# Running sums of the keys' exponentials: from a triangular product on TensorE to a prefix scan on VectorE, with one product of v moved

## The chip, the cores and the metric

The kernel runs on one core of a Trainium2 chip. The metric is the device time of one execution in microseconds (us); lower is better. Within the core, TensorE (PE in the profile; PEld is its weight load), VectorE (DVE), ScalarE (ACT), GpSimd (POOL) and the DMA queues (issued by SyncE, SP) work side by side, each through its own instructions in order, and wait for each other by semaphores.

## The reference

The input has 2 batches of 2048 tokens with 512 features. A gated attention with 64 slots per head (16 heads, key width 64, value width 128) is followed by a layer norm, a gated feed-forward part with a Hadamard transform, and another layer norm. What the change touches is the attention's gating:

```python
z = cumlogsumexp(s, axis=time)            # s = clip(x @ Ws, -32, 32)
g = exp(z[t-1] - z[t])                    # decay of the state
p = exp(s - z)                            # weight of the new token
hk = hk * g + k * p;   ok = q . hk        # keys' state, 64 x 64 per head
pv = softmax(ok)
hv = hv * g + p * v;   ov = pv . hv       # values' state
o = rmsnorm(ov) * gn * silu(x @ Wg);  out = o @ Wo
```

The kernel writes E = exp(s) and keeps the states unscaled. The running sum over time Z of E then enters only as a factor 1/Z on the scores ok and again on the softmax's result. So each chunk of tokens needs Z at every token and slot, its reciprocal, and the last Z of the chunk for the next chunk.

## The kernel before

The attention part walks over `NG` = 4 groups of four heads, and in each over 16 chunks of 128 tokens, both batches together: 64 steps (`Step`). The feed-forward part follows. All is in fp32.

One call of `run` works on four steps at once: `new` loads its input, `now` does its projections and keys' part, `before` does its values' part, and `old` finishes its output product and stores its rows. The kernel writes out the order of PE, DVE, ACT and POOL by hand (a manual schedule), so `run`'s body is the order in each engine's queue, as far as each line uses that engine.

The projections are Strassen-like: a product is seven smaller ones, numbered 1 to 7. `q(k)` makes q, k and s, `v(k)` makes v and the gate, `o(k)` is the output product of an older step. Each accumulates in PSUM banks called `c1` (products 1, 6, 7, 4), `c2` (5, 3) and `c3` (2); `into` then moves a sum out, by ACT (copies `kept`, line 458, and `t`, 460) or by DVE (line 463). For `o`, DVE adds each sum to `rows` (line 742). In a step there are thus two bursts of large products, the seven of q and then v(6), v(5), v(2), v(7), v(3), v(4), with `o` products among them, and between the bursts lies the attention with its small products:

- `exp_s`: DVE clamps s (511); ACT makes `e` (517), and, except in the first chunk of a group, a second exponential `e2` (515), to whose first row POOL adds `zc`, the last running sums of the chunk before (516).
- `k_transposed` (549, copy `kr` 551), `scores` (580), `scores2` (655), `share_of_keys` (590), `share_of_values` (667), `e_transposed` (555, copy `eT` 557), `slots` (608), `state_slots` (617), `values` (678), `state_values` (687).
- `running_sum`: PE multiplies E with a triangular matrix `causal` (562), in a bank of the `c1` kind; ACT copies the result to `z` (564), and two DMAs carry its last row to `zc`. Its second half of columns has the two halves of the tokens swapped (`causal3`).
- `reciprocal` in two halves on DVE (573), each 128x256, one ahead of the values' part, one within v's burst.
- `gated`: ACT squares the values' result (704), DVE multiplies (706) and sums (708), POOL scales (710 to 713).
- `softmax`: DVE multiplies the scores with 1/Z into `r` (625), takes the maximum (631) and subtracts (633); ACT takes the exponential (634). `softmax_sum` sums on DVE and multiplies with 1/Z on POOL (640).
- `o_transposed`: PE transposes (730), ACT copies to `ob` (427, 428), DVE makes two differences (432, 433). Then `o(1)`, `o(5)`, `o(2)` run, and the next call of `run` begins with its q burst.

In the last group, `row_stats` (lines 86 to 91) and `normalize` (95) are done on an old step's rows, the second `row_stats` and `normalize` right after `running_sum`.

The part of the order in `run` that the change touches is, before:

```python
do(now, "exp_s");  ...;  main("v", 1);  ...
do(now, "k_transposed");  do(old, "o", 4);  ...
do(now, "e_transposed");  do(now, "running_sum")
```

Of the kernel before, what the change touches and what calls it, by code (L numbers as in the profile page):

```python
# [9 lines left out]
F32 = mybir.dt.float32  # L10
AF = mybir.ActivationFunctionType
ALU = mybir.AluOpType
# [3 lines left out]
P = 128  # L16
# [5 lines left out]
M = 64  # L22
HG = 4
NG = H // HG
NQ = 4
TH = P // 2
HALVES = (slice(0, TH), slice(TH, P))
# [11 lines left out]
def gated_slot_attention_ffn_kernel(  # L39
# [13 lines left out]
    nc = tc.nc  # L53
# [6 lines left out]
    const = ctx.enter_context(tc.tile_pool(name="const", bufs=1))  # L60
    small = ctx.enter_context(tc.tile_pool(name="small", bufs=4))
    ident = const.tile([P, P], F32, name="ident")
    make_identity(nc, ident)


    causal3 = const.tile([P, P + TH], F32, name="causal")
    causal = causal3[:, 0:P]
    make_upper_triangular(nc, causal, val=1.0, diag=True)
    nc.gpsimd.tensor_copy(causal3[:, P:], causal3[:, 0:TH])
    mhalf = const.tile([P, 2 * NQ], F32, name="mhalf")  # L70
    nc.gpsimd.memset(mhalf, -0.5)
    gn = const.tile([P, 1], F32, name="gn")
# [51 lines left out]
    pch = ctx.enter_context(tc.tile_pool(name="pch", bufs=1, space=PSUM))  # L124
# [23 lines left out]
    xb, acc, res, h, wt = {}, {}, {}, {}, []  # L148
# [203 lines left out]
    with ExitStack() as att:  # L352
        keep = att.enter_context(tc.tile_pool(name="keep", bufs=1))
        c2 = att.enter_context(tc.tile_pool(name="c2", bufs=2))
        c1 = att.enter_context(tc.tile_pool(name="c1", bufs=1))
# [7 lines left out]
        def bank(at, width=P):  # L363
            return ps[at // 2][:, at % 2].rearrange("p (i t) -> p i t", t=width)
# [15 lines left out]
        hk = [keep.tile([P, NQ, M], F32, name=f"hk{s}") for s in range(3)]  # L380
        hv = [keep.tile([P, NQ, DV], F32, name=f"hv{s}") for s in range(2)]

        zc = keep.tile([1, NQ, P], F32, name="zc")
        xd = [dram.tile([P, 7, 2, P], F32, name=f"xd{n}") for n in range(NCB)]

        QUARTERS = [(i, j, HALVES[j], s, HALVES[s], HALVES[s ^ j]) for i in range(NQ) for j in range(2) for s in range(2)]
        OPENS = (1, 2, 5)

        def settle(sums):

            nc.scalar.copy(small.tile([P, 1], F32, name="seen", bufs=1), sums)
# [71 lines left out]
        class Step:  # L465
# [31 lines left out]
            def multiply_q(self, out, k):  # L497
                wt = w["qks"].t
                for c in range(2):
                    xk, wk_ = self.xb[:, RIGHT[k], c, :], wt[:, LEFT[k], c, :]  # L500
                    for i in range(3):
                        a, b = (wk_[:, i * P : (i + 1) * P], xk) if i < 2 else (xk, wk_[:, 2 * P :])
                        nc.tensor.matmul(  # L503
                            out[:, i * P : (i + 1) * P], lhsT=a, rhs=b,
                            start=(k in OPENS and c == 0 and i == 0), stop=(c == 1), skip_group_check=True,
                        )

            def exp_s(self):

                self.e = self.e2 = c2.tile([P, NQ, P], F32, name="e")  # L510
                nc.vector.tensor_scalar(self.e, self.t1[:, :, 2 * P :], -CLAMP, CLAMP, ALU.max, ALU.min)
                if not self.first:

                    self.e2 = c1.tile([P, NQ, P], F32, name="e2", tag="e2")
                    nc.scalar.activation(self.e2, self.e, AF.Exp)  # L515
                    nc.gpsimd.tensor_tensor(self.e2[0:1], self.e2[0:1], zc, ALU.add)  # L516
                nc.scalar.activation(self.e, self.e, AF.Exp)


# [7 lines left out]
            def multiply_v(self, out, k):  # L527
                for c in range(2):
                    nc.tensor.matmul(  # L529
                        out, lhsT=self.xb[:, RIGHT[k], c, :], rhs=w["vg"].t[:, LEFT[k], c, :],  # L530
                        start=(k in OPENS and c == 0), stop=(c == 1), skip_group_check=True,
                    )
# [24 lines left out]
                nc.scalar.copy(self.eT.rearrange("p (j i) t -> p j i t", j=2), pe)  # L557

            def running_sum(self):
                p = pch.tile([P, 512], F32, name="running", tag="c1", bufs=2).rearrange("p (i t) -> p i t", t=P)  # L560
                for j, h in enumerate(HALVES):
                    nc.tensor.matmul(p[:, :, h], lhsT=(causal, causal3[:, TH:])[j], rhs=self.e2[:, :, h], start=True, stop=True)
                z = c1.tile([P, NQ, P], F32, name="z", tag="z")
                nc.scalar.copy(z, p)  # L564
                self.z = z
                if not self.final:
                    for at, h in zip((P - 1, TH - 1), HALVES):
                        nc.sync.dma_start(out=zc[:, :, h], in_=z[at : at + 1, :, h])
                self.iz = c1.tile([P, NQ, P], F32, name="iz")

            def reciprocal(self, half):
                h = slice(2 * half, 2 * half + 2)
                nc.vector.reciprocal(self.iz[:, h], self.z[:, h])  # L573


            def scores(self):
# [119 lines left out]
            def gated(self):  # L696

                sq = c1.tile([P, 2, NQ, DV], F32, name="sq", tag="big")
                self.gj = self.t2[:, :, HD:].rearrange("p q (j d) -> p j q d", d=DV)

                every = slice(0, P)
                moves = [(0, every, every), (1, HALVES[0], HALVES[1]), (1, HALVES[1], HALVES[0])]
                for j, to, at in moves:
                    nc.scalar.activation(sq[to, j], self.po[j][at], AF.Square)  # L704
                for j, to, at in moves:
                    nc.vector.tensor_tensor(self.gj[to, j], self.po[j][at], self.gj[to, j], ALU.mult)  # L706
                ss = small.tile([P, 2 * NQ], F32, name="ss")
                nc.vector.tensor_reduce(ss, sq.rearrange("p j q d -> p (j q) d"), AX.X, ALU.add)  # L708
                self.state()
                nc.gpsimd.tensor_scalar(ss, ss, 1.0 / DV, EPS, ALU.mult, ALU.add)  # L710
                nc.gpsimd.tensor_tensor(ss, ss, mhalf, ALU.pow)
                ssb = ss.rearrange("p (j q o) -> p j q o", j=2, o=1).to_broadcast([P, 2, NQ, DV])
                nc.gpsimd.tensor_tensor(self.gj, self.gj, ssb, ALU.mult)
# [30 lines left out]
            def multiply_o(self, out, k):  # L744
                for c in range(2):
                    nc.tensor.matmul(  # L746
                        out, lhsT=self.ob[:, RIGHT[k], c, :], rhs=w["o"].t[:, LEFT[k], c, :],
                        start=(k in OPENS and c == 0), stop=(c == 1), skip_group_check=True,
                    )
# [248 lines left out]
        def run(new, now, before, old):  # L998


            def do(step, name, *args):
                if step is not None:
                    getattr(step, name)(*args)

            def main(name, k):

                if now is not None:
                    getattr(now, name)(k)
                elif before is not None:
                    for _ in range(FILL[name, k]):  # L1010
                        next(ups)

            def work_on(place):

                if not changes:
                    y["place"] = place
                    next(pieces[0], None)
# [5 lines left out]
            def more():  # L1023

                if old is not None and old.g == NG - 1 and old.n >= NCB - 4:
                    work_on(1)
# [47 lines left out]
                f(0)  # L1074
            if opens:
                w["vg"] = nw.pop("vg")
            main("v", 1)
            more()
            do(before, "load_rows")
            do(now, "k_transposed")  # L1080
            do(old, "o", 4)
# [9 lines left out]
            do(now, "share_of_keys")  # L1091
            do(before, "share_of_values")
            do(now, "e_transposed")
            do(now, "running_sum")
            do(old, "row_stats", 0)
            do(old, "normalize")
# [26 lines left out]
            if o_last:  # L1123
                nw["o"].sums(0, nc.gpsimd)
                nw["o"].sums(1, nc.gpsimd)
            main("v", 7)
            do(now, "softmax")
            main("v", 3)
            more()
# [32 lines left out]
        with tc.manual_schedule(  # L1162
            engines={mybir.EngineType.PE, mybir.EngineType.DVE, mybir.EngineType.Activation, mybir.EngineType.Pool}
        ):
            steps[0].load_x()
            nw["qks"] = load_qks(0)
            steps[1].load_x()
            nw["vg"] = load_vg(0)
            nw["o"] = load_o(0)
            steps[0].make_x()  # L1170
            for k in range(4):
                nw["qks"].sums(k)
            N = len(steps)
            for i in range(N + 2):
                if i == N:
                    open_x("wvg", OUTER[3:], 4 * P)
                    open_acc("ux", tag="h1")
                    ups = up(0, h)
                run(*(steps[j] if 0 <= j < N else None for j in (i + 1, i, i - 1, i - 2)))
            for _ in pieces[0]:  # L1180
                pass
# [6 lines left out]
    with tc.manual_schedule(  # L1188
# [11 lines left out]
        for u in range(NU):  # L1200
            if u:
                h = {}
# [89 lines left out]
```

## Time and profile before

| what | value |
|---|---|
| median of 3 runs | 3518.95 us (3515.03 to 3519.06) |
| profiled execution, its own time | 3517.86 us |
| profiled execution, span from first to last instruction | 3516.1 us |
| busy in the span: TensorE / VectorE / ScalarE / GpSimd | 98% / 67% / 27% / 33% |
| granted TensorE clock, mean | 0.999 |
| running sum on TensorE (line 562) | 256 records of 0.379 us |
| its copy by ScalarE (564) | 64 of 0.587 us |
| reciprocals on VectorE (573) | 128 of 1.75 us |
| GpSimd's additions of zc (516) | 60 of 1.27 us |

The attention part takes about the first 2440 us, the feed-forward part the rest. Busy time is a share of the span. A record of a matmul reaches from its start to a modelled end, and the next one starts before that end; so what a product takes of TensorE's queue is the distance from its start to the next start.

### The profile page before, as it was taken

What the parts mean: (1) busy time and instruction counts of PE and PEld (TensorE: products, weight loads), DVE (VectorE), ACT (ScalarE), POOL (GpSimd) and SP (SyncE); (2) the same over time, 40 slices, a digit from 0 to 9 for tenths busy, and PEclk for the clock granted to TensorE, in tenths of its full rate; (3) what the DMA queues carried; (4) which work ended last, traced back from release to release, by engine and by line L of the source; (5) the groups of instructions that cost most, each with busy time, mean ns of one, the idle gap of its engine ahead of it and who ended that gap; (6) DMA issues with size and microseconds to landing.
All of it is one profiled execution on the core that took longest, in us unless ns stands there. A gap on an engine that the chain in (4) does not pass through costs nothing. (4 is left out here: it accounts for less than half of the span.)

```text
span 3516.1 us, 75258 instructions
## 1 busy us (share of the span) xinstructions
PE 3456.7 (98%) x31840; PEld 2702.8 (77%) x31840; DVE 2354.9 (67%) x3940; ACT 957.0 (27%) x1712; POOL 1144.2 (33%) x1069
## 2 busy tenths in 40 slices
PE   8999999999999999999999999998999999999998
PEld 6777777677777677677777777776888888888887
DVE  5777776665666765656766677777666756756756
ACT  3333333333333333333333333332111111111110
POOL 1222223221221331221332222223634643643544
PEclk9999999999999999999999999999999999999999
DMA  5334334221122232122222243347555544445431
GB/s 184 118 113 138 118 119 152 93 72 62 55 66 70 94 96 65 52 66 70 74 99 68 69 140 129 102 160 270 171 179 205 174 161 176 156 151 184 163 135 68
DMA packets 208833, 425.03 MB, mean 121 GB/s; under 512 B 19696, under 2 KB 120432, under 8 KB 207472
## 3 DMA queue, kind: packets, MB, share of 16 engines
q1 hardware_dynamic: 208496, 420.22, 35.7%
q8 instruction: 250, 4.10, 0.5%
q14 instruction: 87, 0.71, 0.1%
HBM read 297.47 MB, written 125.30 MB: 120 GB/s over the span
## 5 line engine op out<-in xcount | busy, mean ns | idle before, releaser
L529 PE MATMUL c<-wvg,xb 128*128 128x512 f32 x1792 | 812.7, 598 | 4.0 <-DVE wvg L412 2.0
L529 PEld LDWEIGHTS c<-wvg,xb 128*128 128x128 f32 x1792 | 322.1, 190 | 369.6 <-issue 291.9
L503 PE MATMUL c<-xb,wqks 128*128 128x128 f32 x3584 | 553.2, 277 | 15.7 <-DMA wqks<-wqks_blocks 9.6
L503 PEld LDWEIGHTS c<-xb,wqks 128*128 128x128 f32 x3584 | 479.9, 193 | 43.7 <-DVE rows L742 21.5
L218 DVE TENSOR_TENSOR accux<-c,accux 128x512 f32<-128x512 f32 x496 | 341.4, 691 | 180.9 <-PE c L237 163.5
L276 PE MATMUL dc<-w2t,hid 128*128 128x256 f32 x1792 | 455.3, 379 | 2.1 <-DVE res L283 2.1
L237 PE MATMUL c<-wvg,xb 128*128 128x256 f32 x1792 | 432.0, 380 | 6.1 <-DVE accux L218 5.3
L742 DVE TENSOR_TENSOR rows<-c,rows 128x256 f32<-128x256 f32 x448 | 181.7, 418 | 335.9 <-PE c L746 331.4
L237 PEld LDWEIGHTS c<-wvg,xb 128*128 128x128 f32 x1792 | 338.8, 190 | 56.9 <-DVE accux L218 9.1
L276 PEld LDWEIGHTS dc<-w2t,hid 128*128 128x128 f32 x1792 | 340.2, 190 | 49.5 <-DVE res L283 3.3
L503 PE MATMUL c<-wqks,xb 128*128 128x128 f32 x1792 | 347.4, 276 | 0.0
L463 DVE TENSOR_TENSOR t<-c,kept 128x384 f32<-128x384 f32 (+1 forms) x384 | 230.6, 611 | 155.6 <-PE c L503 147.5
L237 PE MATMUL c<-wqks,xb 128*128 128x256 f32 x1344 | 325.1, 380 | 5.2 <-DVE accux L218 2.3
L458 ACT COPY kept<-c 128x384 f32<-128x384 f32 (+1 forms) x384 | 203.5, 530 | 457.8 <-PE c L503 369.5
L516 POOL TENSOR_TENSOR e<-e,zc 1x512 f32<-1x512 f32 x60 | 76.4, 1273 | 710.0 <-ACT e L515 710.0
L237 PEld LDWEIGHTS c<-wqks,xb 128*128 128x128 f32 x1344 | 253.9, 190 | 44.0 <-DVE accux L218 5.0
L503 PEld LDWEIGHTS c<-wqks,xb 128*128 128x128 f32 x1792 | 273.0, 193 | 0.0
L283 DVE TENSOR_TENSOR res<-dc,res 128x256 f32<-128x256 f32 x448 | 189.2, 423 | 117.9 <-PE dc L276 107.3
L573 DVE RECIPROCAL iz<-z 128x256 f32<-128x256 f32 x128 | 223.9, 1749 | 44.6 <-ACT z L564 44.6
L710 POOL TENSOR_SCALAR ss<-ss 128x8 f32<-128x8 f32 x64 | 12.7, 198 | 685.3 <-DVE ss L708 685.3
L706 DVE TENSOR_TENSOR t<-po,t 64x512 f32<-64x512 f32 (+1 forms) x192 | 131.6, 685 | 95.6 <-ACT sq L704 94.3
L252 POOL TENSOR_TENSOR accw<-accw,accux 128x512 f32<-128x512 f32 x64 | 80.8, 1276 | 275.7 <-DVE accux L218 274.3
(189 smaller groups left out, 4975.7 us busy)
## 6 DMA issues: line engine op xcount, KB each, us to landing
xb<-w13s SPq DMA_DIRECT2D x112, 896.0 KB
xb<-xd SPq DMA_DIRECT2D x48, 896.0 KB
yd<-rows SPq DMA_DIRECT2D x128, 256.0 KB
w2t<-w2s SPq DMA_DIRECT2D x32, 896.0 KB
rows<-yd SPq DMA_DIRECT2D x100, 256.0 KB
xd<-xb SPq DMA_DIRECT2D x16, 896.0 KB
wvg<-fxd SPq DMA_DIRECT2D x16, 896.0 KB
w13s<-inner SPq DMA_DIRECT2D x96, 128.0 KB
```

What stands on the lines that cost most here:

```text
L218: nc.vector.tensor_tensor(into[:, b], s, (into if first is None else first)[:, b], ALU.add)
L237: nc.tensor.matmul(s[:, j * TQ : (j + 1) * TQ], lhsT=w[:, LEFT[k], j, :], rhs=right[:, RIGHT[k], :], start=(k in (1, 2, 5) and j == 0), st ...
L252: (nc.gpsimd if u or m == 6 else nc.vector).tensor_tensor(o, o, t["u"][:, b], ALU.add)
L276: nc.tensor.matmul(s, lhsT=h["hid"][:, i, LEFT[m], k * P : (k + 1) * P], rhs=h["w2"][:, i, RIGHT[m], :], start=(m in (1, 2, 5) and i == 0) ...
L283: nc.vector.tensor_tensor(r, s, r, ALU.add)
L458: nc.scalar.copy(self.kept[k], s)
L463: nc.vector.tensor_tensor(t[:, to], s, self.kept[other], ALU.add)
L503: nc.tensor.matmul(out[:, i * P : (i + 1) * P], lhsT=a, rhs=b, start=(k in OPENS and c == 0 and i == 0), stop=(c == 1), skip_group_check=True,
L529: nc.tensor.matmul(out, lhsT=self.xb[:, RIGHT[k], c, :], rhs=w["vg"].t[:, LEFT[k], c, :], start=(k in OPENS and c == 0), stop=(c == 1), sk ...
L573: nc.vector.reciprocal(self.iz[:, h], self.z[:, h])
L706: nc.vector.tensor_tensor(self.gj[to, j], self.po[j][at], self.gj[to, j], ALU.mult)
L742: nc.vector.tensor_tensor(y_, self.uo.sum(k), y_, ALU.add)
```

## The change

The running sums are no longer a product. The transposes of E, which the kernel makes anyway (`eT`, slots on partitions, tokens along the row), are scanned along the tokens by VectorE: `tensor_tensor_scan` computes state = state * 1 + E, once per pair of heads and batch (four instructions of 128x128 each), and starts from `zl`, the last sums of the chunk before, one number per partition. The reciprocals are taken of these transposed sums (`izT`) by the same two instructions as before. Four transposes on TensorE turn them back (`sums_transposed`, put between v(7) and v(3)), and ScalarE copies them to `iz` in three pieces, which swaps the two halves of the tokens for the second half of the columns. ScalarE also copies `zl`. Out go the second exponential, GpSimd's addition, the product with `causal`, ScalarE's copy of `z`, and the two DMAs per step. v(1) moves from ahead of `k_transposed` to behind `e_transposed`.

```diff
             def exp_s(self):
-                self.e = self.e2 = c2.tile([P, NQ, P], F32, name="e")
+                self.e = c2.tile([P, NQ, P], F32, name="e")
                 nc.vector.tensor_scalar(self.e, self.t1[:, :, 2 * P :], -CLAMP, CLAMP, ALU.max, ALU.min)
-                if not self.first:
-                    self.e2 = c1.tile([P, NQ, P], F32, name="e2", tag="e2")
-                    nc.scalar.activation(self.e2, self.e, AF.Exp)
-                    nc.gpsimd.tensor_tensor(self.e2[0:1], self.e2[0:1], zc, ALU.add)
                 nc.scalar.activation(self.e, self.e, AF.Exp)
...
             def running_sum(self):
-                p = pch.tile([P, 512], F32, name="running", tag="c1", bufs=2).rearrange("p (i t) -> p i t", t=P)
-                for j, h in enumerate(HALVES):
-                    nc.tensor.matmul(p[:, :, h], lhsT=(causal, causal3[:, TH:])[j], rhs=self.e2[:, :, h], start=True, stop=True)
-                z = c1.tile([P, NQ, P], F32, name="z", tag="z")
-                nc.scalar.copy(z, p)
-                self.z = z
-                if not self.final:
-                    for at, h in zip((P - 1, TH - 1), HALVES):
-                        nc.sync.dma_start(out=zc[:, :, h], in_=z[at : at + 1, :, h])
-                self.iz = c1.tile([P, NQ, P], F32, name="iz")
+                self.z = z = c1.tile([P, NQ, P], F32, name="z", tag="z")
+                for i in range(NQ):
+                    nc.vector.tensor_tensor_scan(
+                        z[:, i], ones, self.eT[:, i], 0.0 if self.first else zl[:, i : i + 1], ALU.mult, ALU.add
+                    )
+                self.izT = c1.tile([P, NQ, P], F32, name="izT", tag="e2")
             def reciprocal(self, half):
                 h = slice(2 * half, 2 * half + 2)
-                nc.vector.reciprocal(self.iz[:, h], self.z[:, h])
+                nc.vector.reciprocal(self.izT[:, h], self.z[:, h])
+                if half and not self.final:
+                    nc.scalar.copy(zl, self.z[:, :, P - 1])
+            def sums_transposed(self):
+                for i in range(NQ):
+                    nc.tensor.transpose(bank(0)[:, i, :], self.izT[:, i, :], ident)
+                self.iz = c1.tile([P, NQ, P], F32, name="iz")
+                for j, to, at in MOVES:
+                    m = slice(j * M, (j + 1) * M)
+                    nc.scalar.copy(self.iz[to, :, m], bank(0)[at, :, m])
...
                 w["vg"] = nw.pop("vg")
-            main("v", 1)
-            more()
             do(before, "load_rows")
             do(now, "k_transposed")
             do(old, "o", 4)
...
             do(now, "e_transposed")
+            main("v", 1)
+            more()
             do(now, "running_sum")
             do(old, "row_stats", 0)
             do(old, "normalize")
...
             main("v", 7)
+            do(now, "sums_transposed")
             do(now, "softmax")
             main("v", 3)
```

`MOVES` is the list of three moves that `gated` had of its own: all partitions for the first half of the columns, and the two halves of the partitions crossed for the second.

More of the change, by code (lines that the diff above doesn't have):

```diff
@@ L63, in gated_slot_attention_ffn_kernel @@
     make_identity(nc, ident)
-    causal3 = const.tile([P, P + TH], F32, name="causal")
-    causal = causal3[:, 0:P]
+    causal = const.tile([P, P], F32, name="causal")
     make_upper_triangular(nc, causal, val=1.0, diag=True)
-    nc.gpsimd.tensor_copy(causal3[:, P:], causal3[:, 0:TH])
+    ones = const.tile([P, P], F32, name="ones")
+    nc.gpsimd.memset(ones, 1.0)
     mhalf = const.tile([P, 2 * NQ], F32, name="mhalf")
@@ L381, in gated_slot_attention_ffn_kernel @@
         hv = [keep.tile([P, NQ, DV], F32, name=f"hv{s}") for s in range(2)]
-        zc = keep.tile([1, NQ, P], F32, name="zc")
+        zl = keep.tile([P, NQ], F32, name="zl")
         xd = [dram.tile([P, 7, 2, P], F32, name=f"xd{n}") for n in range(NCB)]
@@ L389, in gated_slot_attention_ffn_kernel @@
         OPENS = (1, 2, 5)
+        MOVES = [(0, slice(0, P), slice(0, P)), (1, HALVES[0], HALVES[1]), (1, HALVES[1], HALVES[0])]
         def settle(sums):
@@ L699, in gated @@
                 self.gj = self.t2[:, :, HD:].rearrange("p q (j d) -> p j q d", d=DV)
-                every = slice(0, P)
-                moves = [(0, every, every), (1, HALVES[0], HALVES[1]), (1, HALVES[1], HALVES[0])]
-                for j, to, at in moves:
+                for j, to, at in MOVES:
                     nc.scalar.activation(sq[to, j], self.po[j][at], AF.Square)
-                for j, to, at in moves:
+                for j, to, at in MOVES:
                     nc.vector.tensor_tensor(self.gj[to, j], self.po[j][at], self.gj[to, j], ALU.mult)
```

## The prediction

> **What bounds the kernel now.** I read the page's first rows, then the busy times by stretch, the waits, and three pieces of the timeline.
>
> ```profile
> span 3516.1 us, 75258 instructions
> PE 3456.7 (98%) x31840; PEld 2702.8 (77%) x31840; DVE 2354.9 (67%) x3940; ACT 957.0 (27%) x1712; POOL 1144.2 (33%) x1069
> ...
> 700.00:1300.00 600.00, 595.08 (x6709) 440.09 (x6708) 387.57 (x602) 201.96 (x379) 152.87 (x137) 1.00 0.23 73
> ```
>
> The last line is a stretch of attention: 600 us, then the busy time of PE, PEld, DVE, ACT, POOL, and PE's granted clock (1.00). PE is busy for 595 of 600. The attention part ends near 2440 us; the change touches nothing after it. So the currency is PE's queue: an instruction taken from it is worth its issue time, and a new wait at its head costs its whole length. The waits view says where PE's slack is thin:
>
> ```profile
> PEld c L746 <- ACT ob L427: 47.8, 64, 2.1
> ```
>
> In all 64 steps the weight load of o's first product waits for ScalarE's copy ob (47.8 us in all). That is the weight loader, not yet PE, but nothing is left between them. Now a step of the second group around q's and v's bursts; columns are start, duration, engine, line:
>
> ```profile
> 1470.70 1.03 PE L746 MATMUL c<-wo__11903,ob 128*128 128x256 f32 x4
> 1471.57 1.88 PE L529 MATMUL c<-wvg,xb 128*128 128x512 f32 x4
> 1471.77 0.42 DVE L742 TENSOR_TENSOR rows<-c,rows 128x256 f32<-128x256 f32 x1 [1.65 <-PE c L746]
> ...
> 1473.29 0.60 PE L549 MATMUL ps<-ident,t 128*128 128x128 f32 x4
> 1473.72 1.03 PE L746 MATMUL c<-wo__11903,ob 128*128 128x256 f32 x4
> 1474.68 0.69 PE L580 MATMUL ps<-t 64*64 64x64 f32 x32
> ...
> 1477.26 0.66 PE L555 MATMUL ps<-ident,e 128*128 128x128 f32 x4
> 1477.75 1.03 PE L562 MATMUL running<-e,causal 128*128 128x256 f32 x4
> ...
> 1478.71 0.46 PE L608 MATMUL ps<-e,a 64*64 64x64 f32 x16
> ```
>
> PE durations overlap (the end is modelled), so I cost PE by start to next start: o(7) 0.87, v(1) 1.72, k's transposes 0.43, o(4) 0.96, e's transposes 0.49, the running sum 0.96. DVE finishes reading o(7)'s sum at 1472.19, 1.49 after o(7) began; v(1) hides this. The same step's end:
>
> ```profile
> 1487.91 1.75 DVE L573 RECIPROCAL iz<-z 128x256 f32<-128x256 f32 x1
> 1489.57 1.22 DVE L463 TENSOR_TENSOR t<-c,kept 128x512 f32<-128x512 f32 x2
> 1490.71 0.68 DVE L625 TENSOR_TENSOR r<-ps,iz 128x512 f32<-128x512 f32 x1
> ...
> 1492.94 0.63 ACT L634 ACTIVATE r<-r 128x512 f32<-128x512 f32 x1 [5.84 <-DVE r L633]
> 1493.47 0.57 ACT L427 COPY ob<-ps 128x512 f32<-128x512 f32 x1
> ...
> 1494.10 2.86 PE L746 MATMUL c<-wo__11903,ob 128*128 128x256 f32 x12
> ```
>
> DVE runs back to back into r; ScalarE's exponential waits for r, the copy ob is queued behind that exponential, and o(1) starts 0.06 after ob ends (1494.04). o(1) is also exactly one product (1.72) after v(4)'s start: two chains end together. Last, a step of group 3, where rows are normalized too:
>
> ```profile
> 2115.73 0.69 DVE L86 BATCH_NORM_STATS2 st<-rows 128x6 f32<-128x512 f32 x1
> ...
> 2117.59 1.00 DVE L95 TENSOR_SCALAR rows<-rows,mv,lrs 128x512 f32<-128x512 f32 x2 [0.95 <-POOL lrs L91]
> 2118.50 1.75 DVE L573 RECIPROCAL iz<-z 128x256 f32<-128x256 f32 x1
> 2118.95 1.82 ACT L704 ACTIVATE sq<-po 128x512 f32<-128x512 f32 x3 [1.22 <-PE po L687]
> 2120.16 2.06 DVE L706 TENSOR_TENSOR t<-po,t 128x512 f32<-128x512 f32 x3
> ```
>
> ScalarE's first square ends at 2119.55, but L706 starts at 2120.16: DVE is late, and v(5) needs the bank that L706 reads.
>
> **The change, part by part.** Per step, against the profiled execution's 3517.86 us.
>
> *Removed from PE:* the running sum, 0.96 (four issues of 0.22 and 0.09 of waiting for eT's copy). *Added to PE:* four transposes. Row: e's transposes have records of 0.273 but start 0.109 apart, so 0.44. [...] A full product ahead of slots may cost the 0.1 that o(4) shows ahead of scores; I take 0.05.
>
> *v(1) moved past k's transposes, o(4), scores and the shares.* Its 1.72 is unchanged, and now covers eT's copy. What loses cover: k's transposes need t1, ready 0.68 after o(7) starts, and come at 0.87: no wait. Then o(4) comes at 1.30, but accumulates onto the bank that DVE still reads for o(7), until 1.49; with 0.05 of release that is a wait of 0.24 (0.4 if the weight load starts only then). Scores, shares and e's transposes follow o(4), and stand 1.48 earlier instead of 1.72. kr is no further wait: with one exponential gone from ScalarE it is ready at 3.15, its product comes at 3.48.
>
> *ScalarE, POOL, SP:* out go z's copy (0.59), one exponential (0.63), 60 POOL additions (1.27 each; POOL idled 710 us before them) and 120 DMA issues of zc (SP's queue; nobody waited for zc). In come zl's copy (0.16, beside v's burst) and three copies of iz. Except for iz none is waited for soon: 0.
>
> *The detour of iz.* Before, r needed only DVE. Now: v(7) starts at 0, transposes at 1.72 (the second reciprocal ends at 1.64, just in time), the copies start 0.69 later as for eT, 2.41. A 128x256 copy is 0.37 (hk's row); three, each 0.01 to 0.03 after the last as the three squares stand: 3.55. r starts at 3.57 instead of 2.69, +0.88. Behind r are queued DVE's maximum, v(3)'s sum and ob's sums; ScalarE's exponential and ob; then o(1) and o(5). o(5) moves by +0.88; PE itself explains 0.44, the other 0.44 is waiting. If the copies overlap by 0.1, as ob's two do, it is 0.23 less.
>
> *The scan.* No row shows it. Nearest: DVE's 128x128 addition of two SBUF operands (L886) at 0.284. Reading a scalar per partition costs 0.13 more (normalize 0.545 against clamp 0.417, both 128x512); back to back gives 0.08 back. Four: 1.31. [...] Ends: 0.80 (an addition, no scalar fee) and 3.5 (the reciprocal's 6.3 ns an element). [...] In groups 0 to 2 this is hidden: DVE waits there for ScalarE's squares, with room until the scan reaches 2.9. In group 3 DVE is already late. L706 ends its first third x later, v(5) moves from 6.54 to 8.38 after e's transposes, where PE alone would have it at 6.93: a stall of 1.45 where 0.42 was, +1.03. r loses another 0.1 there (before 2.59). At the row's 1.31 the stall grows by only 0.50.
>
> *Sum.* Groups 0 to 2: -0.52 + 0.05 + 0.24 + 0.44 = +0.21; 50 steps, +10.5. Group 3, where an old step normalizes, 14 steps: +0.21 + 1.03 + 0.1 = +1.34, +18.8. Together +29; with the row's scan +22. 3517.86 + 29 = 3547; the median is 1.1 above the profiled execution, so 3548.
>
> **Rivals.**
> *PE decides (faster).* Should both turnarounds (L742 ahead of o(4), iz ahead of r) fit into slack that I don't see, only -0.52 + 0.05 stays, 64 times: 3489. For it: PE waits for almost nothing in the trace. Point of decision: r must start 0.44 sooner than I reckon, and L742 end 0.24 sooner, and the scan stay under 0.8 in group 3. Against: o(1) stands 0.06 behind ob in nearly every step. 0.10.
> *One turnaround fits.* Overlapped copies and a scan near 0.8: groups 0 to 2 at -0.02 and group 3 at about +0.1: 3520, no change. 0.10.
> *A slow scan.* At 3.5 even groups 0 to 2 stall, by 0.4 at v(5): 50 x 0.63 + 14 x 3.0 = +74, 3593. [...] 0.10.
> *My forecast:* 0.70; its own range is 3525 (scan 1.31, copies overlapping) to 3570 (o(4) waiting 0.4, scan 2.3, 0.2 more in iz).
>
> **Numbers.** A measurement of this kernel can tell about 0.2%, 7 us, from no change. Faster is the first rival and a sliver: 0.11. Same is the second rival and the lowest edge of the forecast: 0.12. Slower: 0.77. The range leaves out the first rival and the slow half of the third: 3514 to 3588.
>
> **What would show it.** Right: in the timeline after, o(4) starts about 1.54 after o(7) behind L742; r waits for ScalarE's iz, about 3.6 after v(7); o(1) some 0.4 late behind ob; four scans take about 1.8; in group 3 v(5) waits over 1 us for L706. L562's group is gone. Wrong: o(1) one product behind v(4) with no wait, a scan record under 0.3 or over 0.8, or group 3's steps growing no more than the others.

## The result and the profile after

The changed kernel takes 3548.57 us (median of 4 runs, 3544.24 to 3551.85), the kernel before 3517.86 on the same chip (4 runs, 3515.03 to 3519.06): a ratio of 1.0087, 95% interval 1.0072 to 1.0102. It is slower, by about what was forecast. The profiled execution is the fastest of the four, 3544.24 us.

The page of the changed kernel and its stretch of attention in the middle (columns as before: length, then busy PE, PEld, DVE, ACT, POOL, clock):

```profile
span 3542.0 us, 75337 instructions
...
PE 3451.3 (97%) x31840; PEld 2687.9 (76%) x31840; DVE 2451.3 (69%) x4196; ACT 959.8 (27%) x1840; POOL 1065.7 (30%) x1009
...
700.00:1300.00 600.00, 587.86 (x6689) 434.24 (x6692) 407.60 (x661) 200.01 (x407) 131.73 (x120) 1.00 0.23 73
```

TensorE's busy time is a little less, yet the span is 25.9 longer. In 600 us it is now idle for 12 where it was idle for 5, at the same clock. The waits of the changed kernel say for whom (total us, how many times, the longest):

```profile
PEld c L748 <- ACT ob L428: 72.1, 64, 2.0
...
PE c L748 <- ACT ob L428: 19.7, 63, 1.2
...
PE c L748 <- DVE rows L744: 10.1, 56, 0.6
```

The first line had 47.8 before. The other two were 5.0 us in 8 waits and 0.6 in one: o(1) now waits for ob in 63 steps, and o(4) for DVE in 56. A step of the second group, from o(7) on (L744 is the sum into `rows`, L545 k's transposes, L584 scores, L551 e's transposes, L525 a product of v, L612 slots):

```profile
1479.78 1.03 PE L748 MATMUL c<-wo__12036,ob 128*128 128x256 f32 x4
...
1480.65 0.60 PE L545 MATMUL ps<-ident,t 128*128 128x128 f32 x4
1480.85 0.42 DVE L744 TENSOR_TENSOR rows<-c,rows 128x256 f32<-128x256 f32 x1 [1.65 <-PE c L748]
...
1481.42 1.10 PE L748 MATMUL c<-wo__12036,ob 128*128 128x256 f32 x4 [0.17 <-DVE rows L744]
1482.45 0.69 PE L584 MATMUL ps<-t 64*64 64x64 f32 x32
...
1485.03 0.66 PE L551 MATMUL ps<-ident,e 128*128 128x128 f32 x4
1485.52 1.88 PE L525 MATMUL c<-wvg,xb 128*128 128x512 f32 x4
...
1486.34 1.61 DVE L559 TENSOR_TENSOR_SCAN z<-ones,zl,eT 128x128 f32<-128x128 f32 x4
1487.33 0.70 PE L612 MATMUL ps<-e,a 64*64 64x64 f32 x32
```

DVE has read o(7)'s sum at 1481.27, and o(4) starts at 1481.42, 1.64 after o(7). k's transposes take 0.77 of the queue instead of 0.44, so the wait is 0.33 (the timeline names 0.17 of it: it counts from the last transpose's end, which is modelled). The same step's end:

```profile
1497.25 0.60 PE L573 MATMUL ps<-ident,izT 128*128 128x128 f32 x4
1497.68 1.88 PE L525 MATMUL c<-wvg,xb 128*128 128x512 f32 x4
1497.93 1.13 ACT L577 COPY iz<-ps 128x256 f32<-128x256 f32 x3 [3.23 <-PE ps L573]
1499.09 0.69 DVE L629 TENSOR_TENSOR r<-ps,iz 128x512 f32<-128x512 f32 x1 [0.79 <-ACT iz L577]
...
1500.28 1.88 PE L525 MATMUL c<-wvg,xb 128*128 128x512 f32 x4
...
1501.80 0.57 ACT L428 COPY ob<-ps 128x512 f32<-128x512 f32 x1
...
1502.42 2.86 PE L748 MATMUL c<-wo__12036,ob 128*128 128x256 f32 x12 [0.26 <-ACT ob L428]
```

v(7) began at 1495.53 (1.72 ahead of the transposes), so r starts 3.56 after it; before, 2.69. From v(4) to o(1) it is 2.14 instead of one product's 1.72. A step of group 3:

```profile
2133.83 1.61 DVE L559 TENSOR_TENSOR_SCAN z<-ones,zl,eT 128x128 f32<-128x128 f32 x4
...
2137.18 1.00 DVE L94 TENSOR_SCALAR rows<-rows,mv,lrs 128x512 f32<-128x512 f32 x2 [0.95 <-POOL lrs L90]
...
2137.76 1.98 PE L525 MATMUL c<-wvg,xb 128*128 128x512 f32 x4
...
2138.10 1.75 DVE L566 RECIPROCAL izT<-z 128x256 f32<-128x256 f32 x1
2139.76 2.05 DVE L708 TENSOR_TENSOR t<-po,t 128x512 f32<-128x512 f32 x3
...
2140.45 5.42 PE L525 MATMUL c<-wvg,xb 128*128 128x512 f32 x12 [0.70 <-DVE t L708]
```

ScalarE's first square ends at 2138.50 (its group starts at 2137.90), L708 only starts at 2139.76, and TensorE stands 0.70 idle ahead of v(5). By start to start v(5) comes 2.69 after v(6), 0.97 beyond one product; in groups 0 to 2 it is 0.10.

For the experiments I use one more measure, worked out from the traces: how much longer the way from one step's e-transposes to the next step's is than in the kernel before, as the median over the steps of groups 0 to 2 and over those of group 3, in us. The changed kernel has +0.37 and +1.12.

### The profile page after: what moved, and what is told of

Read it like the earlier page. It is cut to its first block, busy times and chain, and to the rows that moved or that the text cites. A ratio compares the mean times of both kernels' runs of the same rounds, so it can differ in the third digit from the quotient of the medians.

```text
span 3542.0 us, 75337 instructions
## 1 busy us (share of the span) xinstructions
PE 3451.3 (97%) x31840; PEld 2687.9 (76%) x31840; DVE 2451.3 (69%) x4196; ACT 959.8 (27%) x1840; POOL 1065.7 (30%) x1009
## 5 line engine op out<-in xcount | busy, mean ns | idle before, releaser
L525 PE MATMUL c<-wvg,xb 128*128 128x512 f32 x1792 | 821.7, 597 | 11.2 <-DVE t L708 9.6
L525 PEld LDWEIGHTS c<-wvg,xb 128*128 128x128 f32 x1792 | 315.0, 190 | 338.2 <-issue 260.2
L744 DVE TENSOR_TENSOR rows<-c,rows 128x256 f32<-128x256 f32 x448 | 181.7, 418 | 254.9 <-PE c L748 248.2
L566 DVE RECIPROCAL izT<-z 128x256 f32<-128x256 f32 x128 | 222.7, 1740 | 0.0
L708 DVE TENSOR_TENSOR t<-po,t 64x512 f32<-64x512 f32 (+1 forms) x192 | 131.5, 685 | 98.4 <-ACT sq L706 97.1
L644 POOL TENSOR_TENSOR r<-r,iz 128x512 f32<-128x512 f32 x64 | 83.3, 1302 | 259.0 <-DVE sm L642 259.0
```

The source lines that it names most:

```text
L525: nc.tensor.matmul(out, lhsT=self.xb[:, RIGHT[k], c, :], rhs=w["vg"].t[:, LEFT[k], c, :], start=(k in OPENS and c == 0), stop=(c == 1), sk ...
L566: nc.vector.reciprocal(self.izT[:, h], self.z[:, h])
L644: nc.gpsimd.tensor_tensor(self.r, self.r, self.iz, ALU.mult)
L744: nc.vector.tensor_tensor(y_, self.uo.sum(k), y_, ALU.add)
```

## The experiments

The theory: TensorE does save 0.5 us a step, and three waits take more than that back (o(4) behind DVE's sum, r behind the detour of iz, v(5) behind DVE in group 3). The main rival: VectorE's added load (2354.9 to 2451.3 us) costs wherever it lies. Each run was timed beside the kernel before on its own chip; the medians of that kernel there are 3517.1 to 3519.2 us, so a difference between two rows is uncertain by a few us.

| kernel | us | to before, 95% | groups 0 to 2 | group 3 |
|---|---|---|---|---|
| changed | 3548.6 | 1.0072 to 1.0102 | +0.37 | +1.12 |
| v1_back | 3585.5 | 1.0174 to 1.0205 | +0.69 | +2.41 |
| v1_alone | 3538.3 | 1.0043 to 1.0073 | +0.39 | +0.17 |
| o4_later | 3539.6 | 1.0048 to 1.0081 | +0.30 | +1.05 |
| recip_first | 3535.6 | 1.0033 to 1.0063 | +0.35 | +0.14 |
| scan_twice | 3605.6 | 1.0229 to 1.0261 | +0.64 | +3.19 |
| r_from_izT | 3506.9 | 0.9955 to 0.9979 | -0.41 | +0.58 |
| order_only | 3517.3 | 0.9988 to 1.0005 | -0.06 | +0.13 |
| best | 3498.6 | 0.9930 to 0.9954 | -0.34 | -0.15 |
| best_late | 3487.8 | 0.9903 to 0.9930 | -0.58 | -0.15 |
| before_late | 3504.9 | 0.9958 to 0.9983 | -0.24 | -0.23 |

**v(1) back in its old place (v1_back).**

```diff
+            main("v", 1)
+            more()
             do(before, "load_rows")
...
             do(now, "e_transposed")
-            main("v", 1)
-            more()
```

> The change with v(1) back ahead of k's transposes. Theory (waits): the wait of o(4) for L742 goes (-0.34 a step), but slots must now wait for eT's copy: from e's transposes to slots 1.45 instead of 2.30 with 1.72 of v(1) taken out, +0.87. Net +0.53 in groups 0 to 2 (50 steps, +26). In group 3 VectorE sets v(5) from e's transposes on, which stand 1.38 later: +1.4 x 14 = +19. Together about +45 against the change: 3593. Rival (VectorE's added load is what costs, wherever it lies): v(1)'s place adds no VectorE work, so as the change, 3548 within 5.

Slower by 37 us, not by 45: the direction and the place hold, the size in groups 0 to 2 was 0.32 against the change instead of 0.53. The waits of this kernel show the new one:

```profile
PE ps L612 <- ACT eT L553: 43.2, 64, 0.7
```

slots waits 0.7 in every step for eT's copy. e's transposes to slots is 1.33, less than the 1.45 that I had taken from the kernel before; and o(4) was dearer than its wait (below). So with the scan on VectorE v(1)'s move gains more than o(4)'s new wait costs: eT's copy needs the cover. VectorE's work is the same here, and the load rival, which said 3548, is out for this run.

**v(1)'s move alone, the running sum left on TensorE (v1_alone).**

```diff
-            main("v", 1)
-            more()
             do(before, "load_rows")
...
             do(now, "e_transposed")
+            main("v", 1)
+            more()
```

> The kernel before with only v(1) moved behind e's transposes; the running sum stays on TensorE. Theory: +0.34 for o(4)'s wait, -0.09 for eT's copy now covered: +0.25 x 50 = +12; in group 3 the small products come later by v(1), so that VectorE is no longer late: +0.25 - 0.4, about -2. Together +10: 3528. Rival (o(4)'s wait is absorbed later in the step): no change or faster, 3513 to 3518.

3538.3 for 3528: it costs more than I expected, +0.39 a step in groups 0 to 2 for +0.25, and the rival (no loss) is out. o(4) shows the wait of the changed kernel: 0.33, and 0.07 more up to scores:

```profile
1411.59 1.10 PE L746 MATMUL c<-wo__11895,ob 128*128 128x256 f32 x4 [0.17 <-DVE rows L742]
1412.62 0.69 PE L580 MATMUL ps<-t 64*64 64x64 f32 x32
...
1417.41 1.03 PE L562 MATMUL running<-e,causal 128*128 128x256 f32 x4
...
1418.36 0.69 PE L608 MATMUL ps<-e,a 64*64 64x64 f32 x32
```

The running sum still takes 0.95 up to slots although eT's copy ended 1.9 ahead of slots. So the 0.09 that I had called a wait for eT is no such wait; it stands at the step from a large product to the 64x64 ones.

**o(4) behind scores (o4_later).**

```diff
-            do(old, "o", 4)
...
             do(now, "scores")
+            do(old, "o", 4)
             do(before, "scores2")
```

> The change with o(4) behind scores instead of ahead of them. Theory: o(4) then comes 1.82 after o(7), past the 1.54 at which its bank is free, so its wait of 0.34 a step goes, less up to 0.1 for one more switch between large and small products: -0.24 to -0.34 in 62 steps, -15 to -21 against the change: 3527 to 3533. Rival (the wait only moves to kr or to VectorE's multiplication of the scores): as the change, 3548 within 4.

3539.6 for 3527 to 3533, a miss: the step shrank by 0.07, not by 0.24 to 0.34. o(4) no longer waits:

```profile
1401.52 0.60 PE L545 MATMUL ps<-ident,t 128*128 128x128 f32 x4
...
1402.05 0.69 PE L584 MATMUL ps<-t 64*64 64x64 f32 x32
...
1402.67 1.13 PE L748 MATMUL c<-wo__12052,ob 128*128 128x256 f32 x4
...
1403.73 0.69 PE L659 MATMUL ps<-rT,eT 64*64 64x64 f32 x32
1404.25 0.65 PE L594 MATMUL pk<-e,kr 64*64 64x64 f32 x32
```

But by start to start the transposes take 0.53, scores 0.62, o(4) 1.06, scores2 0.52, where with one change between large and 64x64 products fewer beside them they take 0.44, 0.52, 0.96 and 0.47 in the changed kernel or the one before. So here each such change costs 0.05 to 0.1 on either side of it, and this order has two more: 0.34 of the 0.40 (0.33 and 0.07) that o(4)'s wait had taken. The run's 9 us are more than 62 steps of 0.07; in the two traces the difference is 6.0. The rest is no more than the four runs of the changed kernel differ by among themselves (7.6).

**The first reciprocal ahead of normalize (recip_first).**

```diff
+            do(now, "reciprocal", 0)
             do(old, "normalize")
             do(old, "store_rows")
-            do(now, "reciprocal", 0)
```

> The change with the first half of the reciprocals ahead of normalize on VectorE. Theory: in group 3 VectorE waits 0.95 for GpSimd ahead of normalize, and the reciprocal fills that: L706 about 0.95 sooner, v(5)'s wait for it (0.98 in the profile of the change) all but gone: -0.7 to -0.95 in 14 steps, -10 to -13 against the change: 3536; groups 0 to 2 as in the change. Rival (VectorE's load as such costs): the load is the same, so 3548 within 4.

3535.6 for 3536. Group 3 falls from +1.12 to +0.14, below groups 0 to 2, because in the kernel before group 3 already waited 0.32 a step in v's burst and that goes too; groups 0 to 2 stay. The reciprocal now fills the time in which GpSimd works for normalize:

```profile
2020.15 1.72 DVE L566 RECIPROCAL izT<-z 128x256 f32<-128x256 f32 x1
...
2021.76 3.70 PE L525 MATMUL c<-wvg,xb 128*128 128x512 f32 x8
2021.79 0.90 DVE L94 TENSOR_SCALAR rows<-rows,mv,lrs 128x512 f32<-128x512 f32 x2
2021.89 1.82 ACT L706 ACTIVATE sq<-po 128x512 f32<-128x512 f32 x3 [1.22 <-PE po L691]
...
2022.61 0.68 DVE L708 TENSOR_TENSOR t<-po,t 128x512 f32<-128x512 f32 x1
```

VectorE does the same work and the loss of group 3 is gone: it was the place in the queue. That speaks against the load rival a second time.

**Each scan twice (scan_twice).**

```diff
-                for i in range(NQ):
+                for i in (0, 0, 1, 1, 2, 2, 3, 3):
                     nc.vector.tensor_tensor_scan(
```

> The change with each of the four scans issued twice (the second writes the same result). The scan adds 1.53 us of VectorE's time a step (four starts 0.38 apart). Theory (waits): groups 0 to 2 have about 1.4 between the end of the first reciprocal and L706, so they hide it; group 3 pays it in full ahead of L706: +1.5 x 14 = +21, up to +28 if repeated writes are not overlapped; 3569 to 3578. Rival (VectorE's load costs wherever it lies): the same 1.5 in all 64 steps, +98: 3646.

The number missed (3605.6), and so did the rival's (3646). Three reasons. A repeated scan writes what the one before it wrote and doesn't overlap it:

```profile
1428.25 3.69 DVE L559 TENSOR_TENSOR_SCAN z<-ones,zl,eT 128x128 f32<-128x128 f32 x8
```

Eight take 3.69 for four's 1.61, so 2.08 was added and not 1.53. And the room in groups 0 to 2 is 1.44 (in the changed kernel the first reciprocal ends at 1489.60, L708 starts at 1491.04), which 2.08 overruns by 0.64; 0.27 of that reached TensorE in a typical step. Group 3 paid +2.07 a step, all that was added. And three of group 3's steps paid 1.6 to 3.1 more: over the first 20 us of each the granted TensorE clock is 0.83, 0.91 and 0.83, where the changed kernel has 1.00 in all of group 3. That is 7.7 us of the miss; what lowers the clock was not tested. A load that cost wherever it lies would have cost groups 0 to 2 as much as group 3.

**r without iz (r_from_izT).** The first factor of the softmax takes the sums' reciprocals not yet turned back; transposes and copies stay.

```diff
-                    self.iz.rearrange("p q (j m) -> p j q m", j=2), ALU.mult,
+                    self.izT.rearrange("p q (j m) -> p j q m", j=2), ALU.mult,
```

> The change with the softmax's first product taking izT, the reciprocals not yet turned back, in place of iz: the first factor of the softmax is left wrong, transposes and copies stay. Theory: r no longer waits for ScalarE, so o(1) is back one product behind v(4): the 0.43 that v(4) to o(1) has over a product, and 0.1 at o(5) unchanged: -0.43 in 64 steps, -27: 3521. Rival (the four transposes and their copies cost TensorE and ScalarE more than their own time): nothing is gained, 3548 within 4.

It gains 42 us, more than the 27 of the theory: 0.78 a step in groups 0 to 2.

```profile
1395.91 0.60 PE L573 MATMUL ps<-ident,izT 128*128 128x128 f32 x4
...
1396.88 0.68 DVE L629 TENSOR_TENSOR r<-ps,izT 128x512 f32<-128x512 f32 x1
...
1398.94 1.88 PE L525 MATMUL c<-wvg,xb 128*128 128x512 f32 x4
...
1400.66 2.75 PE L748 MATMUL c<-wo__12036,ob 128*128 128x256 f32 x12
...
1403.25 0.61 PE L504 MATMUL c<-xb,wqks 128*128 128x128 f32 x4
```

r is back at 2.69 after v(7), o(1) at 1.72 after v(4): that is the 0.43. The rest lies further on: o(1) to q(1) falls from 2.69 (1502.42 to 1505.11 in the step of the changed kernel above) to 2.59, o(3) from 1.00 to 0.86, q(2)'s first piece from 0.55 to 0.45. Those three waits, 0.34 in all, were there in the kernel before as well. My reading is that VectorE was behind TensorE there too, and that the transposes' 0.44 lets it catch up when r doesn't wait. Group 3 fits: there the changed kernel has only the first of them (0.10), and it gains 0.54. So r's wait for iz costs 0.78 a step in groups 0 to 2, and the rival (transposes and copies cost by themselves) is out.

**Another order (order_only), and the reciprocals turned back in halves (best).** In groups 0 to 2, v(1) goes back and o(4) takes its place as the cover of eT. It is a large product ahead of slots there, as the running sum was.

```diff
+            norms = old is not None and old.g == NG - 1
+            if not norms:
+                main("v", 1)
+                more()
...
-            do(old, "o", 4)
+            if norms:
+                do(old, "o", 4)
...
             do(now, "e_transposed")
-            main("v", 1)
-            more()
+            if norms:
+                main("v", 1)
+                more()
             do(now, "running_sum")
+            if not norms:
+                do(old, "o", 4)
...
+            do(now, "reciprocal", 0)
             do(old, "normalize")
```

> The change in another order: in groups 0 to 2, v(1) ahead of k's transposes again and o(4) behind e's transposes in its place, where it covers eT's copy; in group 3 the order of the change; the first half of the reciprocals ahead of normalize. Theory: o(4) waits for nothing there, no switch between large and small products is added, and slots need not wait: from o(7) to slots about 7.2 where the change has 7.55: -0.37 x 50 = -18; group 3 as with the reciprocal moved, -12. Together -30: 3518. Rival (eT's cover needs the whole 1.72 of a product, or kr is late without o(4)): no gain over the reciprocal's move, 3536.

3517.3 for 3518: -0.41 a step in groups 0 to 2 over recip_first, and level with the kernel before. `best` adds, between v(2) and v(7), the first half's transposes and copies:

```diff
+            do(now, "sums_transposed", 0)
             main("v", 7)
-            do(now, "sums_transposed")
+            do(now, "sums_transposed", 1)
```

> The same order, and the reciprocals turned back in two halves: the first half's two transposes and three copies between v(2) and v(7), the second half's between v(7) and v(3). Theory: copies of 128x128 take about 0.27, so r starts about 3.05 after v(7) instead of 3.57, and the wait of o(1) falls from 0.42 to 0.15 or less: -0.27 to -0.42 in 64 steps against the other order alone, -17 to -27: 3491 to 3501, faster than both kernels. Rival (the wait of r only moves to another operand, or six copies cost ScalarE more than they save): as the other order alone, 3518.

3498.6, within the range: faster than both kernels, by 0.58% than the one before (0.46% to 0.70%).

```profile
1396.16 0.44 PE L574 MATMUL ps<-ident,izT 128*128 128x128 f32 x2
1396.44 1.88 PE L525 MATMUL c<-wvg,xb 128*128 128x512 f32 x4
...
1398.58 0.81 ACT L579 COPY iz<-ps 128x128 f32<-128x128 f32 x3 [1.09 <-PE ps L574]
1399.42 0.69 DVE L631 TENSOR_TENSOR r<-ps,iz 128x512 f32<-128x512 f32 x1 [0.30 <-ACT iz L579]
...
1400.97 1.88 PE L525 MATMUL c<-wvg,xb 128*128 128x512 f32 x4
...
1402.74 1.56 PE L750 MATMUL c<-wo__12140,ob 128*128 128x256 f32 x6
```

Only three copies of 128x128 are left behind v(7): r starts 2.98 after it, and o(1) 1.77 after v(4), a wait of 0.05.

**The waits that were there before (best_late, before_late).** `best_late` is `best` with one more move: two pieces of VectorE's work, the softmax's last product and the gate's, go behind o(2)'s sum. `before_late` is the kernel before with the same move and the first reciprocal ahead of normalize.

```diff
-            do(now, "softmax_end")
...
-            do(now, "silu")
             do(before, "o", 2)
+            do(now, "softmax_end")
+            do(now, "silu")
```

> The faster version (v(1) back, o(4) as eT's cover, the reciprocals turned back in halves) with the end of the softmax and the gate's product behind o(2)'s sum on VectorE. In it o(1) to the next q(1) takes 2.69 where three products of o take 2.59, o(3) waits 0.14 and q(2) 0.10 for sums that VectorE adds late. Theory: those sums then come first, and the 0.24 to 0.34 a step goes: -15 to -22 in 64 steps, 3477 to 3484. Rival (r's transposes or o's transposes in the next call then come late, or POOL does): no gain or a loss, 3498 or more.

> The kernel before, running sum on TensorE, with two moves on VectorE alone: the end of the softmax and the gate's product behind o(2)'s sum, and the first half of the reciprocals ahead of normalize. Theory: the first gives the same 0.24 to 0.34 a step here, -15 to -22, and the second 0.3 in 14 steps, -4: 3493 to 3499; then what the scan itself is worth is the distance to the version above, some 15. Rival (the kernel before has no such waits): 3518.

Both gain 0.24 a step in groups 0 to 2 (0.34 was the upper end; o(1) to q(1) stays at 2.69, only o(3) and q(2) are cured), but best_late gains nothing in group 3, where o(3) and q(2) had no such waits in `best` (o(3) takes 0.87 there, 1.00 in groups 0 to 2), so it misses its range by 4 us and before_late by 6. best_late is the fastest kernel of this study, 0.84% ahead of the kernel before (0.70% to 0.97%). Between the two lie 17 us: that is what the scan is worth in this kernel once hardly anything waits for it, together with the new order. All of it lies in groups 0 to 2 (0.34 a step); in group 3 best_late is 0.08 a step behind before_late. No other order of the kernel before was tried.

## Why the prediction was right

The forecast was +29 us, to 3548. The medians differ by 31, the profiled executions by 26.4. What decided was what the prediction named: TensorE's saving is smaller than the waits for VectorE's sum, for iz and for VectorE in group 3, and order_only, r_from_izT and recip_first, which each take one of the three away, gain in the place that it names. Its terms, one by one:

- *PE's own saving, -0.52:* right, with one name wrong. The running sum's 0.96 is gone, the four transposes take 0.44 (0.109 apart, as e's transposes do). The length of a transpose's record (0.273) is not what the queue pays. The 0.09 in the 0.96 was not a wait for eT: v1_alone keeps it with eT long copied. In its place v(1) now has 1.81 up to slots, so the allowance of 0.05 should have been 0.09.
- *o(4), +0.24:* right in mechanism, too small. The wait is 0.33, the upper half of the range that I gave: I had 0.05 from the end of DVE's reading to o(4)'s start, and it is 0.15 (1481.27 to 1481.42). And 0.07 more goes between o(4) and scores.
- *iz, +0.44 beyond PE's own:* right as a size against the kernel before (r at 3.56 for 3.57, v(4) to o(1) 0.42 over a product). What I missed is that the kernel before already waited 0.34 a step for VectorE further on, which this detour keeps alive; taken away whole, it was worth 0.78.
- *The scan, 1.84:* too large; it is 1.53 (four starts 0.38 apart). No run shows the 1.84, on which v(5)'s 8.38, its stall of 1.45 and the +1.03 rest: it was my estimate, 0.53 above the 1.31 that I had worked out from rows. In its place the runs showed the 1.53, and +0.66 at v(5). In the 1.31 the fee for the per-partition scalar was mis-sized. (Its rounded terms add up to 1.34; that changes nothing.) I took 0.13 from normalize against the clamp, but normalize reads two such scalars (mean and factor) and the scan one: with it a scan takes 0.460, without (in a group's first chunk) 0.400.

```profile
L559 DVE TENSOR_TENSOR_SCAN z<-ones,zl,eT x240: 457/460/486, 55.9 to 2408.9; 128x128 f32<-128x128 f32 x120
L559 DVE TENSOR_TENSOR_SCAN z<-ones,eT x16: 398/400/426, 24.6 to 1826.1; 128x128 f32<-128x128 f32 x16
```

  The columns of times are the least, median and greatest, in ns. Even without that scalar a scan takes 0.116 more than the addition of the same size (0.400 against 0.284); what takes it was not shown.
- *Group 3, +1.03 for v(5):* right in mechanism; from v(6) to the transposes it takes 0.98 longer than in groups 0 to 2, where it was 0.32 longer before: +0.66. Counted as in the prediction, from one product behind v(6), v(5) waits 0.97 and not 1.45. The shorter scan explains 0.31 of the difference and the larger allowance at slots 0.04 (v(6) comes 0.85 later, not 0.81); 0.02 is left. The further 0.1 that I had put on r came, as 0.09, in other places: 0.05 behind o(1) and 0.04 at the transposes ahead of v(4).
- *Hidden in groups 0 to 2:* right for the scan itself; the room was 1.44 beyond the 1.53, so until 2.97 for my 2.9.

So the mechanism was right, but that the sum came so close is luck: its errors cancel. Groups 0 to 2 lose 0.37 in a typical step instead of 0.21, which would be +18 in 50 steps; over the first 50 of these distances it is 14.0, since some steps, mostly at a group's start, lost less or gained. The 13 distances after them lost 14.2 and the rest of the kernel 0.8, instead of 18.8. Ahead of the first e-transposes the changed kernel is 3.2 ahead. That is in part v(1), 1.72, which now comes behind them, and in part the first product of all, which starts at 8.45 us instead of 9.57, when its weights have landed; the rest was not looked into.

## What to carry to other kernels

Where one engine is full, price an edit by what its queue pays, start to next start, and then look at each turnaround that the moved work used to cover. A product of 1.7 us that looked free to move had hidden a bank's reading by VectorE (o(4) then waited 0.33 for it). When a result moves to another engine, its way back (transposes, copies, the queue behind the first user) can cost more than the work saved (here the wait for iz cost 0.78 a step, for 0.52 saved): bring home early what is ready early, and leave only the last piece on the path. And an order by hand can leave idle time ahead of a wait (here 0.95 on VectorE ahead of normalize); before giving up a change, look whether the next independent instruction in the same queue could fill it.

## What the runs showed of the hardware

- Where large products and 64x64 ones meet, TensorE's queue lost 0.05 to 0.1 on either side, whichever came first: transposes 0.44 or 0.53, a product of o 0.87 or 0.96, v(1) 1.72 or 1.81, scores2 0.47 or 0.52. Two more such changes ate most of what o4_later should have gained (0.34 of 0.40).
- A per-partition scalar added about 0.06 to the scan (0.460 against 0.400 with a constant in its place). normalize with two of them took 0.13 more than the clamp with constants (0.545 against 0.417, both 128x512).
- Four scans into different parts of `z` started 0.38 apart, before the one ahead had ended (0.46). A scan that wrote the same part again added about 0.52 (2.08 for the four repeats), more than a record of 0.484 in that run. So VectorE overlapped the neighbours here that write different parts, and not those that write the same.
